# The edges between the stages of a graph network kernel: starts, gaps and the end of its four stages rearranged, and matmuls added that no one reads

## The chip, the cores and the metric

The kernel runs on one core of a Trainium2 chip. The metric is the device time of one execution in microseconds (us), as the median of three runs. The engines are TensorE (PE, with PEld for its weight loads), VectorE (DVE), ScalarE (ACT), GpSimd (POOL) and SyncE (SP). L359 stands for line 359 of the kernel before.

## The reference, cut to what matters

N is 4096 nodes, F 512 features, in H = 4 heads of D = 128. A layernorm with ReLU stands before each of two layers, and each layer's result is added to its input.

```python
# layer 0, both masks are adj
h  = relu(layernorm(x))
Xw = einsum('hnd,hde->hne', heads(h), W)
f1, f2 = Xw @ V[:, 0], Xw @ V[:, 1]
att = softmax over the neighbours of sigmoid(f1[:, :, None] + f2[:, None, :])
Xn  = batchnorm(att @ Xw)
emb = batchnorm(elu(Xn @ Wenc.T + b) + Xn)             # encoder MLP
Yc  = elu((att @ heads(emb)) @ W.T)                    # decoder attention
x   = x + batchnorm(elu(Yc @ Wdec.T + b) + Yc)         # decoder MLP
# layer 1
h = relu(layernorm(x))
feats = einsum('nf,hfo->hno', h, W1)
e_s, e_n = feats @ a_self, feats @ a_neigh
attn = softmax over the neighbours of leaky_relu(e_s[:, :, None] + e_n[:, None, :], 0.2)
x = x + relu(attn @ feats + b)
```

## The kernel before, in words

Everything but the masks (one byte) is float32 and lies transposed, features on the 128 partitions, nodes along the free axis. The stages follow one another: layernorm and projection of layer 0, encoder attention, encoder MLP, products that turn the encoder's result into values (L648), decoder attention, decoder MLP, layernorm and projection of layer 1, and the attention of layer 1 ("gat").

*Attention.* The loop at L313 runs over 8 blocks, for each head h over two halves tb of 2048 target nodes. Inside a block it runs over 32 key blocks j of 128 source nodes. For each j a weight tile `e` of 128x2048 is made from a row of scores and a mask tile and multiplied with the values of head h: four 512-column products into four banks of PSUM (L359). A product is two records in the profile, so one j is eight. The fourth bank is still being read at a block's start, so its products of j=0 and 1 are caught up at j=2 (`EVICT`, L356). In the encoder and the decoder `e` is made by ScalarE's tanh (L435) and exp (L436) and VectorE's product with the mask (L437). In the layer-1 attention it is ScalarE's Relu (L833) and one VectorE instruction (L834). The encoder writes every fifth `e` to DRAM (`KEEP`) and the decoder reads these back instead of making them (L333).

*Pools of weight tiles.* A tile `e` comes from one of two pools. Two buffers (`EP`) are in the pool `keep`, which lives from the first stage to the end of the decoder's attention. The rest are in the pool of the stage, opened when the memory of the stage before is given back: 6 in the encoder, 4 in the decoder, 7 in layer 1 (where both names stand for the stage's own pool). Which pool the next tile comes from is counted by `made`:

```python
            made += 1
            if made % (EP + ebufs) < EP:
                return keep.tile([P, TB], FP, name="e", tag="ek", bufs=EP)
            return spool.tile([P, TB], FP, name="e", bufs=ebufs)
```

*Row sums.* The softmax's denominators are sums of `e` over j. Some tiles are added by VectorE (L379, L381), some by DMAs that accumulate (L373, the tuple `moved`), and some by matmuls with ones on PE (L252, the tuple `by_ones`). At the block's end the sums of VectorE and of the DMAs go through L252 too. The decoder takes no sums; it reads the encoder's inverses back. In the last block the sums are inverted (L419, L420: `inv`, named `dsb` in the profile), spread over all partitions by PE (L425) and multiplied in. There j=31's products already come behind the sums (`early`).

*MLP.* `mlp_block` takes the products o by o and 512-column block ib by ib. The decoder's MLP also does the residual of layer 0 as its hook `between` says: L695 loads a tile `xt` of the input on SP's queue, L696 scales on ScalarE, L697 adds on VectorE, L699 and L701 sum the features up in `S`, L704 or L706 stores to the output. The decoder MLP's bias needs the sums of the weights, 32 one-column matmuls (L682), queued after the decoder attention.

*Projection of layer 1.* `w1x` holds the weights beside their products with the attention vectors (`pw`: 32 two-column records at L726, copied at L728). `centred(ib)` takes the mean with a matmul (L739), subtracts it (L745), makes ReLU and squares on ScalarE (L748, L749, L752) and adds the four squares (L753, one reduction). `deviation` (L759) follows, then eight groups of products (L776), whose values ScalarE copies with the deviation as factor (L781) and whose scores VectorE copies (L782). `store_rows` transposes the scores of one half on PE and writes them as rows to DRAM; `load_row` reads one back on all partitions. For the first half this stands at L790, behind the deviation of the block after.

*Before the layer-1 attention.* The maximum of the scores is taken over columns, transposed, taken again and spread with a ones-matmul (L796 to L805). ScalarE makes the exponentials of the columns `jcol` and then of the row in four parts (L812 to L815), and `rest_of_rows` (L817 to L827), queued at j=1, makes the rows for the other seven blocks.

*Order.* The Tile framework's scheduler sets each engine's order from the order of the program and simulated times of when operands are ready. `tc.issue_after` and the helper `pinned` fix that an instruction comes behind another in the same engine's queue; they add no wait between engines.

## Time and profile before

| | |
|---|---|
| median of 3 runs | 3273.88 us (3273.81 to 3275.61) |
| profiled execution | 3273.59 us, span of the records 3271.8 us |
| mean granted clock of TensorE in the span | 0.992 |

| stage (start to end, us from the span's start) | length | PE busy | DVE busy | ACT busy | clock |
|---|---|---|---|---|---|
| layernorm and projection, layer 0: 0 to 67.11 | 67.11 | 52.19 | 47.82 | 49.89 | |
| encoder attention: to 1053.58 | 986.47 | 951.56 | 944.35 | 960.32 | 0.99 |
| encoder MLP: to 1165.15 | 111.57 | 110.92 | 74.13 | 49.84 | |
| value products, L648: to 1194.63 | 29.48 | 29.48 | 25.13 | 4.03 | |
| decoder attention: to 2083.54 | 888.91 | 886.36 | 518.81 | 814.03 | 0.99 |
| decoder MLP: to 2193.40 | 109.86 | 109.86 | 87.42 | 66.03 | |
| norm and projection, layer 1: to 2338.64 | 145.24 | 135.01 | 82.95 | 82.29 | 0.95 |
| layer-1 attention: to 3254.12 | 915.48 | 909.87 | 886.19 | 568.00 | 0.99 |
| end: to 3271.8 | 17.68 | 10.97 | 9.13 | 5.63 | 0.93 |

The stages are cut at PE's records: a stage begins with its first matmul. The busy times are those of each engine inside the stage, and the clock is the mean that the throttle granted to PE (1.00 is full speed). The gap before a stage lies in the row of the stage before.

### The profile page before, as it was taken

How to read it: one execution, taken by the hardware profiler on the slowest of the kernel's cores; microseconds unless marked ns; L12 is line 12 of the kernel's file. 1: busy time of each engine (PE TensorE's matmuls, PEld its weight loads, DVE VectorE, ACT ScalarE, POOL GpSimd, SP SyncE). 2: the span in 40 equal slices, each digit the busy share in tenths (PEclk: the TensorE clock that was granted, in tenths of full speed). 3: DMA queues.
4: the chain of work that ended last, by engine and by line, in shares of the span. 5: the costliest groups of instructions: out<-in, count | busy, mean ns of one | idle time of the engine just before them, and what ended most of it. 6: DMA issues, size and time to landing. Idle time of an engine off the chain costs nothing.

```text
span 3271.8 us, 26021 instructions
## 1 busy us (share of the span) xinstructions
PE 3196.2 (98%) x8719; PEld 1484.0 (45%) x8719; DVE 2675.9 (82%) x1916; ACT 2600.1 (79%) x1901; POOL 465.7 (14%) x622
## 2 busy tenths in 40 slices
PE   7999999999999999999999999999999999999999
PEld 6334434444444464444444444448644444444443
DVE  6999999999999665656665665586599999999997
ACT  7999999999997449999999999565666666665663
POOL 3001211211210000000000000024312222222221
PEclk9999999999999999999999999999999999999999
DMA  9998988988986023444443444232398999889985
GB/s 208 196 195 228 268 222 225 266 222 230 271 234 157 0 68 126 151 130 136 140 151 127 132 148 133 63 132 79 84 213 214 219 228 244 214 204 236 224 217 135
DMA packets 211151, 578.48 MB, mean 177 GB/s; under 512 B 25069, under 2 KB 28173, under 8 KB 195017
## 3 DMA queue, kind: packets, MB, share of 16 engines
q0 software_dynamic: 67968, 222.51, 35.9%
q1 hardware_dynamic: 126432, 293.72, 27.1%
q10 hardware_dynamic: 16616, 60.60, 4.7%
q8 instruction: 68, 1.11, 0.1%
q14 instruction: 67, 0.54, 0.0%
HBM read 377.10 MB, written 84.29 MB: 141 GB/s over the span
## 4 chain that ended last, share of the span: by engine, by line
PE 73%; DVE 10%; ACT 7%; issue 5%; DMA 5%; POOL 0%; DVEq 0%; ACTq 0%; SPq 0%; POOLq 0%
PE ps L359 58%; PE ps L592 7%; DVE e L437 6%; ACT e L435 4%; PE ps L776 3%; DMA a<-mask 3%; ACT e L436 2%; DVE acc L381 2%; DMA acc<-e 2%; PE den L252 1%; PE ps L356 1%; PE ps L648 1%; PE ps L516 1%; DMA rinvs<-dcol 1%; PE ps L498 0%
## 5 line engine op out<-in xcount | busy, mean ns | idle before, releaser
L359 PE MATMUL ps<-e,R 128*128 128x512 f32 x6048 | 2628.8, 595 | 40.3 <-DVE e L437 32.9
L359 PEld LDWEIGHTS ps<-e,R 128*128 128x128 f32 x6048 | 1147.0, 191 | 1512.8 <-issue 1420.0
L437 DVE TENSOR_TENSOR e<-e,a 128x2048 f32<-128x2048 f32 (+1 forms) x470 | 1052.4, 2261 | 381.3 <-ACT e L436 367.1
L435 ACT ACTIVATE e<-rowb,score 128x2048 f32<-128x2048 f32 (+1 forms) x470 | 912.7, 1968 | 102.1 <-PE ps L359 58.1
L436 ACT ACTIVATE e<-e 128x2048 f32<-128x2048 f32 (+1 forms) x470 | 871.0, 1880 | 6.4
L833 ACT ACTIVATE e<-rowb,nq,jcol 128x2048 f32<-128x2048 f32 x224 | 460.8, 2089 | 269.2 <-DMA w<-e 136.6
L834 DVE SCALAR_TENSOR_TENSOR e<-e,jcol,a 128x2048 f32<-128x2048 f32 (+1 forms) x259 | 593.0, 2332 | 10.8 <-ACT e L833 10.8
L381 DVE TENSOR_TENSOR acc<-acc,e 128x2048 f32<-128x2048 f32 x130 | 297.3, 2287 | 2.1
L381 DVE TENSOR_TENSOR R<-R,e 128x2048 f32<-128x2048 f32 x121 | 278.0, 2298 | 0.0
L373 POOL DMA_DIRECT2D w<-e x178 | 150.3, 847 | 609.4 <-DMA w<-e 383.3
L592 PE MATMUL ps<-R,w 128*128 128x512 f32 x512 | 220.3, 592 | 0.6 <-DVE w L550 0.6
L373 POOL DMA_DIRECT2D acc<-e x144 | 120.4, 880 | 540.8 <-DMA acc<-e 222.9
L277 POOL DMA_DIRECT2D rb<-rinvs x60 | 34.2, 574 | 1062.5 <-DVE R L540 871.6
L592 PEld LDWEIGHTS ps<-R,w 128*128 128x128 f32 x512 | 97.2, 190 | 122.7 <-issue 117.4
L776 PE MATMUL ps<-w1x,hT 128*128 128x260 f32 x512 | 118.5, 391 | 1.8 <-ACT hT L749 1.8
L612 ACT ACTIVATE ex<-ps,bias 128x512 f32<-128x512 f32 x64 | 44.0, 687 | 95.9 <-PE ps L592 78.8
L776 PEld LDWEIGHTS ps<-w1x,hT 128*128 128x128 f32 x512 | 98.7, 194 | 21.6 <-ACT hT L749 3.4
L833 ACT ACTIVATE e<-w,nq,jcol 128x2048 f32<-128x2048 f32 (+1 forms) x35 | 65.7, 1938 | 30.8 <-DMA R<-e 30.8
L614 DVE SCALAR_TENSOR_TENSOR ex<-ex,re 128x512 f32<-128x512 f32 x64 | 45.0, 704 | 36.1 <-ACT re L613 35.9
L781 ACT ACTIVATE R<-ps,rstd 128x128 f32<-128x128 f32 x128 | 38.3, 369 | 38.1 <-PE ps L776 37.0
L787 POOL TENSOR_TENSOR vacc<-vacc,R 128x128 f32<-128x128 f32 x120 | 53.0, 468 | 57.5 <-ACT R L781 57.5
L252 PE MATMUL den<-e,ones 128*32 128x512 f32 x440 | 53.0, 598 | 0.0
(162 smaller groups left out, 1228.6 us busy)
## 6 DMA issues: line engine op xcount, KB each, us to landing
a<-mask SPq DMA_DIRECT2D x720, 256.0 KB, 4.3
w<-e POOLq DMA_DIRECT2D x178, 512.0 KB, 6.6
acc<-e POOLq DMA_DIRECT2D x144, 512.0 KB, 7.0
ekeep<-e ACTq DMA_DIRECT2D x48, 1024.0 KB, 7.4
e<-ekeep SPq DMA_DIRECT2D x48, 1024.0 KB, 4.9
mask<-in_adjT POOLq DMA_DIRECT2D x8, 2048.0 KB, 104.5
rowb<-rows SPq DMA_DIRECT2D x16, 1024.0 KB, 8.0
rb<-rinvs POOLq DMA_DIRECT2D x60, 256.0 KB, 4.5
```

What stands on the lines that cost most here:

```text
L252: last_ones = nc.tensor.matmul(den[s * 32:(s + 1) * 32, :], ones[:, 0:32], t[:, s * IB:(s + 1) * IB], start=start, stop=stop)
L359: last_main = nc.tensor.matmul(b, block(values[h], j), e[:, s * IB:(s + 1) * IB], start=(j == 0), stop=(j == NJ - 1))
L373: nc.gpsimd.dma_start(into_half, e_half, **({"accum_op": ALU.add} if j > moved[0] else {}))
L381: nc.vector.tensor_add(acc, acc, e)
L435: nc.scalar.activation(e, rowb, AF.Tanh, bias=column(score[:, 1], j, h), scale=0.5)
L436: last_act = nc.scalar.activation(e, e, AF.Exp, scale=0.5)
L437: last_dve = nc.vector.tensor_mul(e, e, a)
L592: nc.tensor.matmul(z, w[:, fb, o * P:(o + 1) * P], nodes(src[fb], ib), start=(fb == 0), stop=(fb == C - 1))
L776: nc.tensor.matmul(b[:, 0:2 * DX], hT[:, fb, c * P:(c + 1) * P], w1x[:, fb, 2 * k:2 * k + 2, :].rearrange("p h x -> p (h x)"), start=(fb = ...
L787: nc.gpsimd.tensor_add(vacc[:, h, :], vacc[:, h, :], block(v1[h], j))
L833: last_act = nc.scalar.activation(e, rowb, AF.Relu, bias=column(nq, j, h), scale=column(jcol, j, h))
L834: last_dve = nc.vector.scalar_tensor_tensor(e, e, column(jcol2, j, h), a, ALU.add, ALU.mult)
```

## The change

In the order of the program:

- *Kernel's start.* The statistics of the first 128 nodes are finished by themselves (`deviations(0, 1)`), those of the other three chunks of the first block behind the second chunk's turn.
- *Weight tiles.* With `made - 1` in place of `made`, the first two tiles of every stage come from `keep`, where before only the first did. In the first block of the decoder, j < 8, each j's weights are queued behind the exp (L436) of the j before it.
- *Decoder MLP's bias.* L682 becomes a hook of the decoder attention, queued at j=6 of its second block, and the subtraction at j=16.
- *Gap before layer 1's projection.* L726 is queued behind the MLP's last product, and a matmul of 512 columns (`stay_busy`, whose result is not read) follows each of its four groups. For block 0 the mean is taken of `S` without the last head, and a second matmul adds that head. The first two chunks' products are queued before the deviation, and `centred` of the next block comes one chunk later in block 0.
- *Rest of the projection.* L753 becomes two additions. The first half's rows are stored at chunk 2 of block 4 instead of before block 4. The residuals of head 3 are pinned behind the ReLUs of the block before.
- *Gap before the layer-1 attention.* For the last chunk the scores are copied before the values. The maximum's matmuls and the four of L821 get fillers of 256 and 512 columns behind them. One part of the row is made before the weights, the other three between the parts of the first weights, and the first three tiles are made in four parts (`in_parts0=3`).
- *End.* In the last layer-1 block j=30 and 31 are added by VectorE (L381) instead of L252, and the products of both (`late`) come behind the sums and the inverse. In the encoder's last block only j=31's products come behind the sums, as before.

The diff, with the line of the kernel before at each place and blank lines and comments left out:

```diff
@@ before 68
-GAT_LAST = (3, 5, 7, 9, 11, 13, 15, 17, 19, 21, 23), (12, 30, 31)
+GAT_LAST = (3, 5, 7, 9, 11, 13, 15, 17, 19, 21, 23), (12,)
@@ before 109
+    def stay_busy(behind, n=1, cols=IB):
+        for _ in range(n):
+            with tc.issue_after(behind.ins):
+                behind = nc.tensor.matmul(bank()[:, 0:cols], ident, w0Ts.rearrange("p h d -> p (h d)")[:, 0:cols],
+                                          start=True, stop=True)
+        return behind
@@ before 213
-                  kept=None, sums=None, sums2=None, extras={}, row0=None, masks0=()):
+                  kept=None, sums=None, sums2=None, extras={}, row0=None, masks0=(), in_parts0=1):
@@ before 242
-            if made % (EP + ebufs) < EP:
+            if (made - 1) % (EP + ebufs) < EP:
@@ before 318
-            po, ahead = [bank() for _ in range(SB - 1)], []
+            po, ahead, late = [bank() for _ in range(SB - 1)], [], []
@@ before 325
-                with pinned([a_load, *products_of] if j else []):
+                with pinned([a_load, *products_of, last_main] if j else []):
@@ before 340
-                    products_of = weights(e, rowb, a, j, h, SB if n + j == 0 else 1)
+                    with pinned(products_of[:1] if kept == "read" and n == 0 and j < 8 else []):
+                        products_of = weights(e, rowb, a, j, h, SB if NJ * n + j < in_parts0 else 1)
@@ before 364
-                early = last and j == NJ - 1 and invert is not None
-                if not early:
+                if last and invert is not None and j >= NJ - (1 if kept is not None else 2):
+                    late.append((j, e))
+                else:
@@ before 395
-                if early:
-                    products()
@@ before 409
+            for s, b in enumerate(po):
+                for k, t in late:
+                    nc.tensor.matmul(b, block(values[h], k), t[:, s * IB:(s + 1) * IB], start=(k == 0),
+                                     stop=(k == NJ - 1))
@@ before 473
+                rstd = work.tile([P, C], FP, name="rstd")
@@ before 475
-                with pinned([first_hn] if ib == 1 else []):
-                    for c in range(C):
+                def deviations(lo, hi):
+                    with pinned([first_hn] if ib == 1 or lo == 1 else []):
+                        for c in range(lo, hi):
@@ before 478
-                for c in range(C):
+                    for c in range(lo, hi):
@@ before 480
-                rstd = work.tile([P, C], FP, name="rstd")
-                last_dve = rsqrt(rstd, mv[:, :, 1], LN_EPS)
+                    return rsqrt(rstd[:, lo:hi], mv[:, lo:hi, 1], LN_EPS)
+                last_dve = deviations(0, 1 if ib == 0 else C)
@@ before 483
+                    if ib == 0 and c == 1:
+                        last_dve = deviations(1, C)
@@ before 592
-                    nc.tensor.matmul(z, w[:, fb, o * P:(o + 1) * P], nodes(src[fb], ib),
+                    last = nc.tensor.matmul(z, w[:, fb, o * P:(o + 1) * P], nodes(src[fb], ib),
@@ before 593
+                return last
@@ before 609
-                        product(z, o, ib, 0, C)
+                        last_product = product(z, o, ib, 0, C)
@@ before 622
-                last = bn_coefs(stats, gamma, beta, a_mlp, b_mlp, o, o + 1)
-            return last
+                bn_coefs(stats, gamma, beta, a_mlp, b_mlp, o, o + 1)
+            return last_product
@@ before 666
+        def sums_of_weights(load):
+            banks.append(bank1())
+            for o in range(C):
+                for fb in range(C):
+                    nc.tensor.matmul(banks[1][:, o:o + 1], w[:, fb, o * P:(o + 1) * P], ones[:, 0:1],
+                                     start=(fb == 0), stop=(fb == C - 1))
+        def bias_of_decoder(load):
+            nc.vector.tensor_sub(bias, vec_of("dec_mlp_b"), banks[1][:, 0:C])
@@ before 670
-                      kept="read")
+                      kept="read", extras={(1, 6): sums_of_weights, (1, 16): bias_of_decoder})
@@ before 679
-        pb = bank1()
-        for o in range(C):
-            for fb in range(C):
-                nc.tensor.matmul(pb[:, o:o + 1], w[:, fb, o * P:(o + 1) * P], ones[:, 0:1],
-                                 start=(fb == 0), stop=(fb == C - 1))
-        nc.vector.tensor_sub(bias, vec_of("dec_mlp_b"), pb[:, 0:C])
@@ before 697
-            nc.vector.tensor_add(d, d, xt)
+            added = nc.vector.tensor_add(d, d, xt)
@@ before 700
-            elif o > 1:
+            elif o == C - 2 or o == C - 1 and ib > 0:
@@ before 706
+            return added
@@ before 715
-        last_coefs = mlp_block(work, w, xd, x1, "dec_mlp_bn_gamma", "dec_mlp_bn_beta", None,
+        last_product = mlp_block(work, w, xd, x1, "dec_mlp_bn_gamma", "dec_mlp_bn_beta", None,
@@ before 722
+        last_pe = last_product
@@ before 723
+            with tc.issue_after(last_pe.ins):
@@ before 726
-                nc.tensor.matmul(pw[:, k:k + 2], w1Ts[:, h, fb * P:(fb + 1) * P], a1s[:, h, :], start=True, stop=True)
-        with tc.issue_after(last_coefs.ins):
-            nc.vector.tensor_copy(w1x[:, :, :, D:DX], pw[:, 0:2 * C * H].rearrange("p (c h s) -> p c h s", h=H, s=2))
+                    last_pe = nc.tensor.matmul(pw[:, k:k + 2], w1Ts[:, h, fb * P:(fb + 1) * P], a1s[:, h, :],
+                                               start=True, stop=True)
+            last_pe = stay_busy(last_pe)
@@ before 737
-            residual(C - 1, ib)
+            added = residual(C - 1, ib)
@@ before 738
+            if ib == 0:
+                with tc.issue_after(last_pe.ins):
+                    nc.tensor.matmul(pm, mean_of, S[ib], start=True, stop=False)
+                nc.tensor.matmul(pm, mean_of, nodes(x1[C - 1], ib), start=False, stop=True)
+                with tc.issue_after(added.ins):
+                    nc.vector.tensor_copy(w1x[:, :, :, D:DX],
+                                          pw[:, 0:2 * C * H].rearrange("p (c h s) -> p c h s", h=H, s=2))
+            else:
@@ before 749
-                nc.scalar.activation(hT[:, fb, :], d[:, fb, :], AF.Relu)
+                last_relu = nc.scalar.activation(hT[:, fb, :], d[:, fb, :], AF.Relu)
@@ before 753
-            nc.vector.tensor_reduce(S[ib], sq.rearrange("p c n -> p n c"), AX.X, ALU.add)
-            return hT
+            nc.vector.tensor_add(sq[:, 0:2, :], sq[:, 0:2, :], sq[:, 2:4, :])
+            nc.vector.tensor_add(S[ib], sq[:, 0, :], sq[:, 1, :])
+            return hT, last_relu
@@ before 764
-        hT = centred(0)
+        def values(hT, c):
+            banks = []
+            for k in range(2):
+                banks.append(bank())
+                for fb in range(C):
+                    m = nc.tensor.matmul(banks[k][:, 0:2 * DX], hT[:, fb, c * P:(c + 1) * P],
+                                         w1x[:, fb, 2 * k:2 * k + 2, :].rearrange("p h x -> p (h x)"),
+                                         start=(fb == 0), stop=(fb == C - 1))
+            return banks, m
+        hT, last_relu = centred(0)
+        ahead = [values(hT, c) for c in range(2)]
+        with tc.issue_after(ahead[-1][1].ins):
@@ before 769
-                if c == 1 and ib < NIB - 1:
-                    hT_next = centred(ib + 1)
+                if c == (1 if ib else 2) and ib < NIB - 1:
+                    with pinned([last_relu]):
+                        hT_next, last_relu = centred(ib + 1)
+                if (ib, c) == (SB, 2):
+                    store_rows(rows1[0], targets(0))
+                    row0 = w.rearrange("p c f -> p (c f)")
+                    load_row(row0, rows1[0], 0)
@@ before 772
+                pvs, pvs_last = ahead.pop(0) if ahead else values(hT, c)
@@ before 774
-                    b = bank()
-                    for fb in range(C):
-                        nc.tensor.matmul(b[:, 0:2 * DX], hT[:, fb, c * P:(c + 1) * P],
-                                         w1x[:, fb, 2 * k:2 * k + 2, :].rearrange("p h x -> p (h x)"),
-                                         start=(fb == 0), stop=(fb == C - 1))
-                    pv = heads_of(b)
+                    pv = heads_of(pvs[k])
+                    at_end = j == NJ - 1
+                    if at_end:
+                        nc.vector.tensor_scalar_mul(scores_of(j, k), pv[:, :, D:DX], r)
@@ before 781
+                    if not at_end:
@@ before 790
-            if ib == SB - 1:
-                store_rows(rows1[0], targets(0))
-                row0 = w.rearrange("p c f -> p (c f)")
-                load_row(row0, rows1[0], 0)
+        last_pe = stay_busy(pvs_last, cols=IB // 2)
@@ before 798
-        nc.tensor.transpose(pt[0:H, 0:P], mloc, ident)
+        with tc.issue_after(last_pe.ins):
+            last_pe = stay_busy(nc.tensor.transpose(pt[0:H, 0:P], mloc, ident), cols=IB // 2)
@@ before 804
-        nc.tensor.matmul(pm[:, 0:H], ones[0:H, :], mdiag, start=True, stop=True)
+        with tc.issue_after(last_pe.ins):
+            last_pe = nc.tensor.matmul(pm[:, 0:H], ones[0:H, :], mdiag, start=True, stop=True)
@@ before 809
-        last_act = nc.scalar.activation(jcol, jcol, AF.Exp)
-        nc.vector.tensor_scalar_mul(nq, jcol2, -1.0)
+        last_exp = nc.scalar.activation(jcol, jcol, AF.Exp)
@@ before 812
-        for row, in in_parts(SB, row0):
-            last_dve = nc.vector.tensor_scalar(row, row, mbc[:, 0:1], G_MAX, ALU.add, ALU.min)
-            with tc.issue_after(last_act.ins):
-                last_act = nc.scalar.activation(row, row, AF.Exp, scale=0.8)
+        row_parts = [row for row, in in_parts(SB, row0)]
+        def held(row):
+            nc.vector.tensor_scalar(row, row, mbc[:, 0:1], G_MAX, ALU.add, ALU.min)
+        held(row_parts[0])
+        last_scalars = nc.vector.tensor_scalar_mul(nq, jcol2, -1.0)
@@ before 817
-    def rest_of_rows(load):
@@ before 819
+    with tc.issue_after(last_pe.ins):
@@ before 821
-            nc.tensor.matmul(pss[:, h:h + 1], vacc[:, h, :], ones[:, 0:1], start=True, stop=True)
+            last_pe = nc.tensor.matmul(pss[:, h:h + 1], vacc[:, h, :], ones[:, 0:1], start=True, stop=True)
+    last_pe = stay_busy(last_pe, 3)
+    def rest_of_rows(load):
@@ before 831
+        last_act = last_exp
@@ before 832
+            if row_parts:
+                row = row_parts.pop(0)
+                with tc.issue_after(last_act.ins), tc.issue_after(last_scalars.ins):
+                    if len(row_parts) < SB - 1:
+                        held(row)
+                    nc.scalar.activation(row, row, AF.Exp, scale=0.8)
@@ before 860
+        with tc.issue_after(last_pe.ins):
@@ before 863
-                  (N * TINY, ALU.add), sums=R[2][:, 0:TB], sums2=(row0, R[2][:, TB:N]), row0=row0,
+                      (N * TINY, ALU.add), sums=R[2][:, 0:TB], sums2=(row0, R[2][:, TB:N]), row0=row0, in_parts0=3,
```

## The prediction

> **What bounds the kernel now.** I read the page's first part, then TensorE's (PE's) timeline, the granted clock in short stretches, then VectorE's (DVE's) timeline.
>
> ```profile
> PE 3196.2 (98%) x8719; PEld 1484.0 (45%) x8719; DVE 2675.9 (82%) x1916; ACT 2600.1 (79%) x1901; POOL 465.7 (14%) x622
> ```
>
> PE is busy 98% of the span, so only its 75.6 us of idle time, its stretches at half clock and work taken off it can move the end. The timeline of PE says where these lie (start, length, instruction, count, idle time before it):
>
> ```profile
> 1194.63 2.74 PE L359 MATMUL ps<-e,R 128*128 128x512 f32 x6
> 1197.20 1.02 PE L356 MATMUL ps<-e,R 128*128 128x512 f32 x2
> 1198.06 4.39 PE L682 MATMUL den<-ones,w 128*128 128x1 f32 x32
> 1205.01 5.46 PE L359 MATMUL ps<-e,R 128*128 128x512 f32 x6 [2.55 <-DVE e L437]
> 1210.26 1.37 PE L356 MATMUL ps<-e,R 128*128 128x512 f32 x2
> 1211.47 108.31 PE L359 MATMUL ps<-e,R 128*128 128x512 f32 x252
> ...
> 2193.40 3.63 PE L726 MATMUL den<-a1s,hT 128*128 128x2 f32 x32
> 2201.17 2.04 PE L739 MATMUL ps<-S,mean_of 128*128 128x512 f32 x2 [4.14 <-DVE S L701]
> 2205.02 6.75 PE L776 MATMUL ps<-w1x,hT 128*128 128x260 f32 x16 [1.80 <-ACT hT L749]
> ...
> 2242.65 1.05 PE L759 MATMUL den<-mean_of,S 128*128 128x1 f32 x8 [2.23 <-DVE S L753]
> ...
> 3257.70 3.70 PE L359 MATMUL ps<-e,R 128*128 128x512 f32 x8
> 3261.97 3.70 PE L425 MATMUL ps<-dsb,ident 128*128 128x512 f32 x8 [0.57 <-DVE dsb L420]
> ```
>
> A 512-column matmul is two records of 0.429 us at full clock (252 in 108.2) and twice that at half clock. One key block j of an attention stage is 8 records, 3.43 us. The stretches by window give the clock (second last columns: PEclk, DMA share):
>
> ```profile
> 309.84:313.25 3.41, 1.51 (x4) 0.49 (x3) 3.41 (x4) 3.41 (x3) 0.00 (x0) 1.00 0.00 1
> 794.54:797.95 3.41, 1.61 (x5) 0.68 (x4) 3.41 (x2) 3.41 (x3) 0.00 (x0) 1.00 0.77 317
> 1197.31:1200.72 3.41, 3.41 (x28) 2.93 (x26) 0.00 (x0) 3.41 (x3) 0.00 (x0) 1.00 0.93 332
> 1204.14:1207.55 3.41, 2.54 (x3) 1.17 (x4) 2.92 (x2) 3.41 (x3) 0.00 (x0) 0.50 0.25 79
> ```
>
> The clock falls at 74.3, 313.3, 965.2, 1200.7, 2197.4 and 2340.8 us and rises at 81.2, 316.7, 968.6, 1211.0, 2211.1 and 2351.0. All differences are multiples of 3.413 us (2340.8-1200.7 is 334 of them), so it is decided in windows of that length. PE counted as fully busy in the third window and lost the clock: 2.6 us of it were one-column matmuls. With 1.61 us of 512-column work (the window at 794.54) it held; with 1.51 it fell. A cold window with 2.54 us did not raise it. So only columns streamed count, about 1.5 of 3.41 us hold the clock, and nearly a full window restores it.
>
> Last, VectorE's supply in the layer-1 attention:
>
> ```profile
> 2452.76 11.41 DVE L834 SCALAR_TENSOR_TENSOR e<-e,jcol,a 128x2048 f32<-128x2048 f32 x5
> 2458.91 1.92 PE L252 MATMUL den<-e,ones 128*32 128x512 f32 x16
> ```
>
> The first of these five is block 0's last weight tile, j=31, ready at 2455.1. PE starts on it at 2458.91-3.43, about 2455.4. VectorE is busy for all 103 us from 2356 to 2459. Its lead, some 4 to 5 us at j=20, is down to 0.3 us: PE cannot end this block earlier than VectorE lets it.
>
> **The change part by part**, on the profiled execution's own time, 3273.59 us (span 3271.8); the median is 0.29 above it.
>
> *Decoder attention's start, +4.8.* Two tiles instead of one now come first from the pool that outlives the encoder stage. In the changed program's order ScalarE makes j=1, not j=5, right after the encoder attention (where 1049.5 to 1053.4 held j=5). So both j=0 and j=1 wait ready at 1194.63. ScalarE then makes j=2 from 1194.8: tanh 1.94, exp 1.9, VectorE's mask product 2.3, ready 1201.0; PE wants it at 1194.63+16x0.429=1201.5. j=3 is ready at 1204.9 and wanted at 1204.9; from j=5 on there are 3 us to spare. The order pinned over j<8 keeps ScalarE from pairing tanhs there. Gain: 1211.47-1201.5=9.97. But L682 hid in this gap, and is now queued on PE behind block 1's j=5, in a stage that PE bounds without a gap. Its price by L726, 32 such records in 3.4: 3.45 us. Then the clock: L555's 24 small records (3.04 us from 962.7) lost it for one window, so I add half of 3.41, 1.7. 9.97-3.45-1.7=4.8. Bounds: no clock lost 6.5; two windows and a late j=3, 2.5.
>
> The Trainium skill, "TensorE: Matmul & The Clock Gate", Part 1, says that the clock follows how busy PE has been in free-running windows of some 3.4 us, and advises that no idle gap exceed about 3 us. The grid agrees, at 3.413. By PE's busy row, L682 would keep the clock and the part be worth 6.5; by the window at 1197.31 small matmuls are as good as idle. I follow the trace.
>
> *Gap before layer 1's projection, +3.1.* L726 is cut into four groups of 8 records (0.86 each) with a 512-column filler (0.86) after each: PE runs to 2193.4+6.9=2200.3. All four lie in the wait of 4.14, and half of the stretch streams, 1.6 to 1.7 us per window, barely above the 1.5 that fell. The mean (L739) now takes S without head 3 and then x1[3] itself, dropping VectorE's L701 (0.69) from the chain: one more matmul, both at full clock, done 2202.0. VectorE subtracts from 2202.15 (was 2203.26). ScalarE has one residual (L696) ahead of the first ReLU, not eight, so L776 starts near 2203.6. Sixteen L776 matmuls (0.44 each) follow before the deviation; the squares are added in 1.2+0.7 (between the 0.69 and 2.29 of 512 and 2048 columns). I place block 1's first L776 at 2221.7, against 2225.28: 3.6. In the wait from 2202 to 2206 only three 0.44 us matmuls stream; a window lying there (one phase in three) loses the clock, 0.5 on average. Bounds 1.5 and 4: if the fillers fail to hold the clock they cost nothing, lying in the wait.
>
> *Rest of layer 1's projection, +2.6.* L753's reduction (3.75 us, which PE waited for at 2242.65, 2.23) becomes two adds of 1.9. The transpose of the first half's scores waits no more (0.39 at 2275.6). PE's own period is 15.78 us a block; ScalarE has 11.3, VectorE 8.6 in it. The residuals of blocks 4 to 7 move inside their blocks; on SP the row load now stands between the loads of xt, with a full block of slack. Bounds 0 and 3.
>
> *Gap before layer 1's attention, +1.15.* The last score goes ahead of ScalarE's copies (mloc 0.66 earlier), one row part is finished before the first weights, and the first three key blocks are split in four. First product: 2342.5 against 2344.90. But ScalarE now runs 4 row exps at 0.52, 12 parts at 0.71 and g: from 2340.4 to 2351.2 instead of 2341.0 to 2350.2, so j=3 leaves VectorE 0.9 earlier only (start 2353.3 against 2354.19), because VectorE no longer waits for L821 and the transpose after it (1.16 before 2351.56). From there its queue is full to j=31. PE gains 0.9 and the lead of 0.26. By the skill's rule the gap must not cool PE: 6.1 us at half clock, another 3.05, and the total would be 17.5. By the lead these are handed back as waits for e before j=31; I take 1.15. Bounds 0 and 4.5. Fillers here lie in a wait of 4.99.
>
> *End, +2.6.* The row sums of j=30 and 31 go from L252 (16 records, 1.74) to two more VectorE adds (2x2.23); VectorE ended its last tile at 3241.9, so they are done by 3246.4, five us before the sums. Two products, 6.87 us, now follow the sums, over the inverse's 0.69+3.35: the 0.57 wait and 0.26 of slack go. 1.74+0.83=2.57. Bounds 2 and 2.8.
>
> *Kernel's start, 0.* The first chunk's statistics are finished alone, so its transposes start near 6.4 instead of 9.5; chunks 1 to 3 then follow the second, separate chain, at 9.75, as before. Bounds -1.7 (the clock rises a window later) and +0.5. The encoder attention is unchanged: ScalarE is 99.9% busy there.
>
> Sum 14.3: 3273.88-14.3=3259.6.
>
> **The rivals.** *The fillers decide the second gap* (chance 0.12): PE keeps its 4.5 us. For it: PE was cold for 6 us. Against: the lead. 3256.
> *New waits eat most* (0.10): j=3 late, the clock lost twice, the fillers too sparse. For it: margins of 0.1 us. About 3267.
> *Slower* (0.03): SP's queue holds the residual loads of each block behind stores and the row load, and with two xt tiles the mean waits in every block of the projection. It decides above (11.7+6.5)/7=2.6 us a block; one wait for xt of 2.50 is in the trace (VectorE, 2231.7), hidden there. At 3.5 a block it is 24.5-11.7: 3287. Against: a block of slack.
> *The change does not do what it says*: cold PE in both gaps despite the fillers leaves 12 or 13 of the 14.3; it stays in the main case (0.75), 3255 to 3265.
>
> **How the numbers follow.** 0.2% is 6.5 us, about what can be told from no change. Faster: 0.75+0.12+half of the 0.10, 0.92 with rounding; same 0.05; slower 0.03. The range, 3254.5 to 3265.0, is the main case with most of the first rival.
>
> **What would show it.** Right: L359 unbroken from 1194.6; L682 inside block 1 with the clock falling once after it; L753 gone and no wait at its place; waits for VectorE's e before the end of the first layer-1 block. Wrong: that block without a wait and over 3 us shorter, waits for xt, or a gap at j=3 of the decoder.

## The result, and the profile after

| | before | after |
|---|---|---|
| median | 3275.74 us, 13 runs (3272.27 to 3279.27) | 3265.74 us, 13 runs (3260.23 to 3269.86) |
| ratio | | 0.9968, 95% interval 0.9961 to 0.9975 |
| profiled execution, span | 3273.59, 3271.8 | 3260.23, 3258.4 |

The change saves 10.0 us between the medians; the ratio gives 10.5, with an interval of 8.2 to 12.8. The prediction was 14.3 us and 3259.6, with a range to 3265.0. The direction was right, the size too large, and the time came out 0.7 us above the range. The profiled execution of after is the shortest of its 13, so the 13.4 us between the two profiles flatter the change; a second profile of each follows below.

The page of after, first part:

```profile
PE 3197.5 (98%) x8723; PEld 1484.0 (46%) x8723; DVE 2665.4 (82%) x1933; ACT 2601.8 (80%) x1908; POOL 477.6 (15%) x622
```

PE's busy time has grown by 1.3 us, its idle time has fallen from 75.6 to 60.9 us, and the span has shrunk by 13.4. (A record at half clock counts twice as long in the busy time, so the added fillers and the cold windows that went, windows of 3.413 us at half clock, nearly cancel in it.) PE's timeline in after, at the decoder attention's start and at the moved sums (L371 is the product, L368 the catch-up, L694 the sums):

```profile
1196.54 5.32 PE L371 MATMUL ps<-e,R 128*128 128x512 f32 x12
1201.69 1.88 PE L368 MATMUL ps<-e,R 128*128 128x512 f32 x4
1203.40 17.49 PE L371 MATMUL ps<-e,R 128*128 128x512 f32 x40
1222.21 18.29 PE L371 MATMUL ps<-e,R 128*128 128x512 f32 x42 [1.32 <-DVE e L452]
...
1328.75 3.63 PE L694 MATMUL den<-ones,w 128*128 128x1 f32 x32
1332.24 13.12 PE L371 MATMUL ps<-e,R 128*128 128x512 f32 x30
```

The gap of 2.55 us after j=0 and the sums in it are gone, but a wait of 1.32 us stands five tiles later, before j=7. The gap before layer 1's projection, the gap before its attention, and the end:

```profile
2196.72 1.11 PE L115 MATMUL ps<-w0Ts,ident 128*128 128x512 f32 x2
2197.66 1.02 PE L771 MATMUL ps<-S,mean_of 128*128 128x512 f32 x2
2198.52 1.02 PE L772 MATMUL ps<-x,mean_of 128*128 128x512 f32 x2
2200.98 7.31 PE L809 MATMUL ps<-w1x,hT 128*128 128x260 f32 x32 [1.44 <-ACT hT L787]
...
2330.14 4.52 PE L115 MATMUL ps<-w0Ts,ident 128*128 128x512 f32 x6
2334.49 5.31 PE L371 MATMUL ps<-e,R 128*128 128x512 f32 x12
...
2439.97 3.70 PE L371 MATMUL ps<-e,R 128*128 128x512 f32 x8 [0.76 <-DVE e L904]
2444.44 3.70 PE L371 MATMUL ps<-e,R 128*128 128x512 f32 x8 [0.77 <-DVE e L904]
...
3241.70 7.13 PE L423 MATMUL ps<-e,R 128*128 128x512 f32 x16
3248.68 3.60 PE L440 MATMUL ps<-dsb,ident 128*128 128x512 f32 x8
```

The wait of 4.14 us for the mean is gone and the clock stays up through the fillers (L115), as the same profile's windows from the MLP's last product on show (1.00, third column from the end):

```profile
2190.65:2197.66 7.01, 7.01 (x41) 5.09 (x40) 5.37 (x13) 3.57 (x5) 0.00 (x0) 1.00 0.00 0
2197.66:2208.00 10.34, 8.90 (x37) 6.54 (x36) 5.51 (x8) 5.08 (x9) 0.00 (x0) 1.00 0.20 71
```

In the layer-1 attention PE starts earlier (7.3 us behind the projection's end instead of 7.6, and 5.6 in the second profile, which lost no window there) and then waits twice for VectorE's last tiles of the block, as the prediction said. At the end the two late products run into the spreading without a wait.

The lengths of the stages, from PE's records of all profiles taken (the encoder attention ends with its last product, the two decoder blocks with the third block's catch-up, and the last stretch with the span). "Before" means every profile whose code in that stage is that of the kernel before, "after" likewise; the number of profiles is in brackets.

| stretch | before, mean (range) | after, mean (range) | gain | predicted |
|---|---|---|---|---|
| start, to the encoder's first product | 69.8 (67.1 to 74.7) [6] | 69.3 (68.2 to 71.6) [11] | none clear | 0 |
| encoder attention | 983.6 (982.4 to 985.9) [4] | 984.7 (982.0 to 987.2) [9] | -1.1 | 0 |
| decoder attention, first two blocks | 233.9 (233.3 to 234.9) [3] | 231.9 (230.2 to 233.6) [9] | 2.0 | 4.8 |
| MLP's end to the projection's end | 144.1 (142.6 to 145.2) [5] | 136.4 (136.35 to 136.5) [10] | 7.8 | 5.7 |
| projection's end to the second layer-1 block's catch-up | 129.5 (128.9 to 130.4) [5] | 129.74 (129.73 to 129.75) [7] | -0.2 | 1.15 |
| last layer-1 block's catch-up to the end | 120.25 [5] | 117.7 [12] | 2.55 | 2.57 |

All other stretches agree to 0.01 us from kernel to kernel (the six layer-1 blocks between take 683.82 us in each). The gains sum to 11.0 us, which lies within the interval of the ratio. The ranges of the encoder attention overlap, so its -1.1 is not clear by itself.

### The profile page after: what moved, and what is told of

Same layout as the page of the kernel before. It is cut to its first block, busy times and chain, and to the rows that moved or that the text cites. A ratio compares the mean times of both kernels' runs of the same rounds, so it can differ in the third digit from the quotient of the medians.

```text
span 3258.4 us, 26085 instructions
## 1 busy us (share of the span) xinstructions
PE 3197.5 (98%) x8723; PEld 1484.0 (46%) x8723; DVE 2665.4 (82%) x1933; ACT 2601.8 (80%) x1908; POOL 477.6 (15%) x622
## 4 chain that ended last, share of the span: by engine, by line
PE 68%; ACT 12%; DVE 9%; issue 7%; DMA 3%; POOL 0%; ACTq 0%; DVEq 0%; POOLq 0%
PE ps L371 52%; ACT e L450 7%; PE ps L613 7%; DVE e L452 5%; ACT e L451 4%; PE ps L809 3%; DMA a<-mask 2%; DVE acc L394 2%; PE den L262 1%; DVE e L904 1%; DVE R L394 1%; PE ps L670 1%; DMA acc<-e 1%; PE ps L368 1%; PE ps L537 1%
## 5 line engine op out<-in xcount | busy, mean ns | idle before, releaser
L371 PE MATMUL ps<-e,R 128*128 128x512 f32 x6024 | 2614.1, 594 | 37.5 <-DVE e L452 35.2
L371 PEld LDWEIGHTS ps<-e,R 128*128 128x128 f32 x6024 | 1140.1, 190 | 1504.8 <-issue 1396.6
L613 PEld LDWEIGHTS ps<-R,w 128*128 128x128 f32 x512 | 97.2, 190 | 122.7 <-issue 117.7
L846 POOL TENSOR_TENSOR vacc<-vacc,R 128x128 f32<-128x128 f32 x120 | 65.8, 576 | 45.3 <-ACT R L839 45.0
```

What stands on the lines that cost most here:

```text
L371: last_main = nc.tensor.matmul(b, block(values[h], j), e[:, s * IB:(s + 1) * IB], start=(j == 0), stop=(j == NJ - 1))
L613: last = nc.tensor.matmul(z, w[:, fb, o * P:(o + 1) * P], nodes(src[fb], ib), start=(fb == 0), stop=(fb == C - 1))
L846: nc.gpsimd.tensor_add(vacc[:, h, :], vacc[:, h, :], block(v1[h], j))
```

## The experiments

"Before" runs on the same chip beside every group, and its median differs from chip to chip, so kernels of one group are compared with each other or by their ratio to before.

**The changed kernel again, and the kernel before again.** No edit.

> The changed kernel as it is. Its profile of 3260.23 us is the lowest of its 13 times (median 3265.74), so the 13.4 us between the two profiles are more than the 10.0 between the medians. Theory A (phase): the clock's 3.413 us windows lie differently in each execution; this trace then shows other half-clock windows, mostly at the kernel's start, near 962, after L694 and in the two gaps, each worth up to 1.7 us, and they make up the difference to the first profile; everywhere else the stages agree within 0.3 us. Theory B (supply): the difference lies in the encoder attention, whose blocks 0 to 3 already differ by -1.1 to +0.4 us between the two profiles; then the clock's windows explain under 1 us of it and the blocks before 580 us explain the rest. Expected time 3263 to 3268 us under both.

> The kernel before as it is, for a second profile of it. Theory A (phase): start, gaps and the small-matmul places carry other half-clock windows than the first profile, the encoder's blocks agree within 0.3 us. Theory B (supply): the encoder's first blocks differ by about 1 us each, the stages from 1170 us on agree within 0.3 us apart from single windows of 1.7. Expected 3273 to 3278 us.

Measured: after 3266.01 us (6 runs, 3263.85 to 3266.71; before 3275.1), its profiled execution 3266.62. The 6.4 us between the two profiles of after lie in three places: the encoder attention took 986.4 instead of 982.0, the second decoder block 115.14 instead of 113.44 (one cold window), the rest at the start. So both theories hold a part, and supply holds the larger one. Before's second profile (3273.2) has 983.1 us in the encoder, and 1.6 us less in the decoder's start and 1.4 less before the layer-1 attention than its first: two cold windows in each where the first had three. The prediction had measured its gains against a profile with these extra windows.

**The old start.** `deviations(0, C)` for every block, so that all four statistics come together.

> The changed kernel with only the kernel's start as before (all four statistics of the first block together). In the first profile of the changed kernel the clock rose at 20.2 us instead of 12.9 and the encoder attention began at 69.38 instead of 67.11. Theory A: the split start does this, since its first transposes leave a wait of 2.06 us on PE and no window is full; then this kernel begins the encoder attention near 67.1 and is 1.9 to 2.3 us faster than the changed kernel. Theory B: the window's phase does it; then the begin lies anywhere between 66.5 and 69.5 in both, and the times differ by under 1 us.

Measured: 3266.31 us (6 runs) beside 3266.01 of after on the same chip; its encoder begins at 69.17 us, after's at 69.66. That is theory B, the phase; the old start reaches from 67.1 to 74.7 us in six profiles and the new one from 68.2 to 71.6 in eleven, so the split start shows neither gain nor loss. The 2.3 us that the first profile of after seemed to lose here were one execution's.

**One VectorE addition less in the first layer-1 block.**

```diff
-GAT_FIRST = (0, 2, 4, 6, 8, 10, 12, 14, 16, 18, 20, 22, 24), (30, 31)
+GAT_FIRST = (0, 2, 4, 6, 8, 10, 12, 14, 16, 18, 20, 22, 24, 26), (30, 31)
```

> The changed kernel with j=26 of the first layer-1 block summed by the DMA instead of VectorE (one 2.28 us add less there). Theory A (VectorE's lead bounds this block): the three waits of PE for e (1.8 us together, two of them near j=27 to 31) go, the stretch from the first product to the second block's catch-up (122.40 us in the changed kernel's profile) shrinks by 1.3 to 1.8 us to about 120.8, and the whole by the same. Theory B (the waits come from single tiles' latency or from the DMA sums): the stretch stays within 0.4 us, or grows because the block's sums wait for a later accumulation.

Measured: 3263.16 us (5 runs) beside 3266.01, which so few runs do not tell from chance (the means differ by 1.8); the stage's length does. PE's waits in the block, after (second profile) first and then this kernel (line, what it waited for, us in total, times, longest):

```profile
PE ps L371 <- DVE e L904: 1.8, 3, 0.8
PE ps L193 <- ACT g L890: 1.1, 1, 1.1
...
```

```profile
PE ps L193 <- ACT g L890: 1.1, 1, 1.1
...
PE ps L371 <- DVE e L904: 0.3, 1, 0.3
```

Three waits for `e` become one of 0.3, and the stretch from the projection's end falls from 129.74 to 127.54 us, 2.2 less, about the price of the 2.28 us addition and more than the 1.3 to 1.8 expected. VectorE's lead bounds this block: with the addition its queue is full from the fourth tile to the last, and PE ends when VectorE does.

**No fillers in the first gap; no fillers in the second.** `stay_busy` left out behind L755's groups, and in the other kernel all five fillers before the layer-1 attention: behind the last products, behind the maximum's transpose and behind the sums (L881).

> The changed kernel without the four fillers before layer 1's projection; nothing else differs on PE. Theory A (the fillers hold the clock there): PE's clock falls near the end of the decoder MLP's last products and comes back only about 10 us into the projection; from the MLP's end to the projection's end takes 139 to 142 us instead of 136.4. Theory B (the clock is held anyway or the stretch waits for VectorE and ScalarE): the stretch stays within 0.5 us of 136.4.

> The changed kernel without the five fillers before the layer-1 attention. Theory A (VectorE's lead decides): the clock falls for one to three windows and the first product is later or slower, but from the projection's end to the second block's catch-up still takes 129.7 to 130.2 us (129.7 and 129.8 in two profiles, of which one lost the clock there and one did not); time unchanged. Theory B (the fillers decide this gap): 1.7 to 5 us more in that stretch and in the time.

Measured: without the first, the stretch from the MLP's end to the projection's end is 138.42 us instead of 136.36, so these four fillers are worth 2.06 us by this one profile; ten profiles with them lie between 136.35 and 136.51. The medians are 3266.99 (8 runs) and, without the second, 3265.06 (4 runs); against before (ratios 0.9970 and 0.9964) neither can be told from after's 0.9968. Without the first the clock was lost for three windows (busy time by engine; the third column from the end is PE's clock):

```profile
2201.46:2204.87 3.41, 1.30 (x2) 0.50 (x2) 1.43 (x6) 1.00 (x2) 0.00 (x0) 0.50 0.00 0
2204.87:2208.28 3.41, 1.97 (x4) 0.62 (x3) 2.11 (x4) 1.36 (x3) 0.00 (x0) 0.50 0.45 154
2208.28:2211.70 3.42, 3.42 (x10) 2.65 (x9) 0.74 (x2) 3.42 (x7) 0.00 (x0) 0.50 0.00 0
```

PE was busy in 6.69 of these 10.2 us, so half clock cost 3.3 at most (an estimate, half of 6.69); the rest of them are PE's waits. Why 2.06 of the 3.3 remain was not followed. In the second gap the clock was lost as well, PE's first products ran at half speed, and nothing was lost in time:

```profile
2334.35 8.22 PE L371 MATMUL ps<-e,R 128*128 128x512 f32 x12 [2.53 <-issue]
2342.41 0.27 PE L193 MATMUL ps<-ident,g 128*128 128x128 f32 x1
2342.52 1.88 PE L368 MATMUL ps<-e,R 128*128 128x512 f32 x4
```

The same twelve records took 5.31 us in the first profile of after. Still the stretch to the second block's catch-up is 129.74 us here, and 129.73 and 129.74 in after's two profiles, of which one lost a window and one did not. The fillers of the second gap are worth nothing: what PE loses there it would otherwise wait for later.

**The old reduction.** `tensor_reduce` over the four squares in place of two additions, one run.

> The changed kernel with the squares of layer 1's norm added by the one reduction (3.75 us) instead of two additions (1.23+0.69). From the MLP's end to the projection's end 136.36 us in the changed kernel. Theory A (PE waited for this reduction): once per early block a wait of 1 to 2 us before the deviation comes back, 138.5 to 142 us. Theory B (the new place of the next block's norm and the pinned residuals already give it a block of slack): within 0.5 us of 136.4, except for block 0.

Measured: 138.42 us for the same stretch, so the two additions are worth 2.06 us. Only the first two blocks lose, with waits of 0.37 and 0.28 at block 0 and 1.19 at block 1; from block 2 on there is slack. So neither theory holds whole: the loss is near what A asked for at least, 138.5, but stands in two blocks only.

**The turn alone.** In the kernel before, `made - 1` in place of `made`, and nothing else.

> The kernel before with one edit: made - 1 in place of made, so that two tiles of every stage come from the pool that lives on. On PE only the 16 sums of the decoder's weights (L682) stand behind j=1's products now instead of j=0's. Theory A (the turn alone fills the decoder's start; the moved sums were not needed): the two first decoder blocks, from the first product to the third block's catch-up, take 2x109.87+5.15+3.45 = 228.3 us plus 1.7 per window at half clock, 228 to 232, against 234.9 and 233.3 in two profiles of before and 230.2 to 233.6 with the whole change. Theory B (without the pinned order and the moved sums a later tile is late): 232 or more. For the encoder: theory C (the turn makes its row sums' DMAs late in block 2): the whole encoder attention 982 or 986.5, with a wait of ScalarE near 317 or 340 us after its start and none near 311; theory D (execution alone): a wait near 311 again, 982.4 to 983.1. Time: A and D about 3270, A and C up to 3274.

Measured: PE's timeline at the decoder's start:

```profile
1205.96 5.32 PE L359 MATMUL ps<-e,R 128*128 128x512 f32 x12
1211.11 1.88 PE L356 MATMUL ps<-e,R 128*128 128x512 f32 x4
1212.83 3.63 PE L682 MATMUL den<-ones,w 128*128 128x1 f32 x32
1216.32 34.15 PE L359 MATMUL ps<-e,R 128*128 128x512 f32 x79
```

The two blocks take 228.46 us, 5.4 less than before and 3.4 less than the whole change has on the mean. The sums at their old place fill the time until j=2 is ready, and no window was lost behind them, here or in the other kernel with this code. So the moved sums and the pinned order do not help; they take back a good part of what the turn gives. But the median of this kernel is 3274.65 (13 runs), 1.0 below before (ratio 0.9997, 0.9989 to 1.0006). What became of the other four us was open after it. Its encoder took 986.1.

**The encoder in the old turn.** `made - (kept != "write")`: old turn in the encoder attention, new one elsewhere.

> The changed kernel, but in the encoder attention the weight tiles come from the two pools in the old turn (made instead of made - 1); the order on every engine stays. In three of four profiles with the new turn the encoder attention from its first product to its last took 986.0 to 987.2 us (the first one 982.0), in two of before 982.4 and 983.1; the difference lies in the third block (124.6 to 124.7 against 121.7 and 122.3). Theory A (the turn decides which buffers the row sums' DMAs read and hold): the encoder attention goes back to about 983, its third block to 122, and the whole to about 3262.5. Theory B (supply varies from execution to execution): 986 again as often as not, the time stays at 3265 to 3266.

Measured: 983.02 us in the encoder, a wait of ScalarE at 311 us; 3264.47 us (5 runs), in the same group as the two without fillers (3266.99 and 3265.06). By itself this does not settle it, since profiles with the new turn reach 982 too.

**A better kernel, and the same with the old encoder turn.** On top of after: j=26 by DMA, `j < 10` in place of `j < 8` for the pinned tiles, and the sums folded:

```diff
+            ws = spool.tile([P, IB], FP, name="exd", bufs=2)
+            nc.vector.tensor_add(ws, w[:, 0, :], w[:, 1, :])
+            for fb in range(2, C):
+                nc.vector.tensor_add(ws, ws, w[:, fb, :])
             for o in range(C):
-                for fb in range(C):
-                    nc.tensor.matmul(banks[1][:, o:o + 1], w[:, fb, o * P:(o + 1) * P], ones[:, 0:1],
-                                     start=(fb == 0), stop=(fb == C - 1))
+                nc.tensor.matmul(banks[1][:, o:o + 1], ws[:, o * P:(o + 1) * P], ones[:, 0:1], start=True, stop=True)
```

> The changed kernel with three edits: j=26 of the first layer-1 block summed by the DMA (as before: -2.2); the decoder's first eight tiles pinned up to j < 10, so that j=8's tanh no longer passes j=7's (PE waited 1.32 us there); and the decoder bias's weight sums folded over the four row blocks by three VectorE adds of 0.69, which lie in VectorE's slack, so that 8 one-column records are left of 32 (3.45 to 0.86 us) and the clock is not lost after them (1.7 to 3.4 in three of four profiles). Theory A: 2.2+1.3+2.6+1.7, 7.8 us less than the changed kernel, about 3258.2. Theory B: the adds delay the mask products of block 1 or another tile is late at the decoder's start; then only the 2.2 and part of the rest, about 3262.

> The three edits of the better kernel (3257.88) and, in the encoder attention alone, the old turn of the weight tiles. Theory A (the new turn costs the encoder up to 4 us in more than half of the executions): its attention takes 982.4 to 983.2 us, with a wait of ScalarE near 311 us, and the median is 1.5 to 2.5 us lower, about 3256. Theory B (execution alone): the median stays within 1 us of 3257.9, and the encoder may take 986 here too.

Measured: 3257.88 us (5 runs, ratio 0.9940, 0.9927 to 0.9952) and, with the old turn, 3257.29 (5 runs; before 3275.63). The first forecast held to 0.3 us, in part by luck, since it was set from another group's median: by the stages this kernel is 8.2 us shorter than after (5.95 in the decoder's first two blocks, 2.2 in the layer-1 block), where 7.8 were expected. PE's timeline of the better kernel:

```profile
1203.40 36.80 PE L371 MATMUL ps<-e,R 128*128 128x512 f32 x85
...
1327.16 0.95 PE L697 MATMUL den<-ones,exd 128*128 128x1 f32 x8
1327.97 7.54 PE L371 MATMUL ps<-e,R 128*128 128x512 f32 x17
```

With j=8 held back, PE runs on at j=7 without a wait: 115.18 us for the stretch that took 116.76. So the 1.32 us of after were j=8's tanh ahead of j=7's in ScalarE's queue. The folded sums take 0.8 us and lose no window: 110.76 us for the second block against 113.44 to 116.82. With the old turn the encoder took 985.9 in its profile, so it too has long executions, and the medians agree within 1 us: theory B, as far as five runs each tell.

**A lighter third encoder block.** On top of the better kernel; then the same edit in before, in the turn alone and in after.

```diff
+ENC_THIRD = (0, 2, 10, 12, 15, 17, 20, 22, 25), (5, 7, 8, 9, 30, 31)
 ENC = (0, 2, 5, 7, 10, 12, 15, 17, 20, 22, 25), (8, 9, 30, 31)
...
-lambda n: (ENC_FIRST, ENC_SECOND, ENC)[min(n, 2)]
+lambda n: (ENC_FIRST, ENC_SECOND, ENC_THIRD, ENC)[min(n, 3)]
```

> The better kernel (3257.88; its encoder turn is the new one) with a lighter third encoder block: j=5 and j=7 are summed by ones-matmuls on PE instead of the DMA (11 tiles by DMA become 9; 1.74 us more PE work in a block that ScalarE bounds). In eleven profiles so far the third block took 120.7 to 125.0 us, with either turn, and what ScalarE waits for there is the DMA of a row sum (acc<-e), 1.8 to 7.0 us in all; POOL's queue sends these one behind the other and stands 12.1 us behind the small transfer of the denominators and 7.4 to 8.4 behind that of the inverses. Theory A (these sums are late, by how long a transfer takes in that execution): the third block takes 119 to 121 us, ScalarE's waits near 311 to 341 us after the encoder's start are gone or under 1 us, and the median falls by about 2, to 3256. Theory B (the supply of masks, or ScalarE itself, sets the block): 121 to 125 us still, the median within 1 us of 3257.9.

Measured: 3251.57 us (5 runs, 3249.34 to 3252.18; before 3276.69; ratio 0.9922, 0.9908 to 0.9935), the fastest of all. By the ratios it is some 6 us below the better kernel, where about 2 were expected; with five runs of each on different chips the size is rough. What ScalarE waited for in the third encoder block, in the first and in the second profile of after:

```profile
ACT e L450 <- DMA acc<-e: 1.8, 2, 1.1
```

```profile
ACT e L450 <- DMA acc<-e: 5.7, 3, 2.8
```

With the lighter block no such wait is left, and the block takes 119.64 us (120.7 to 125.0 in thirteen profiles without the edit). POOL's queue shows where the two executions of after part, at the same pair of accumulations; the first profile, then the second:

```profile
371.06 1.84 POOL L386 DMA_DIRECT2D acc<-e  x2
378.22 0.85 POOL L386 DMA_DIRECT2D acc<-e  x1 [5.33 <-DMA acc<-e]
```

```profile
372.58 1.84 POOL L386 DMA_DIRECT2D acc<-e  x2
381.62 0.85 POOL L386 DMA_DIRECT2D acc<-e  x1 [7.19 <-DMA acc<-e]
```

The next accumulation goes only when the last has landed. Here it waits 1.9 us longer; the row sums behind it hold their weight tiles as much longer, and ScalarE, which bounds the encoder, waits for a tile.

> The kernel before with the lighter third encoder block (j=5 and 7 summed by PE instead of the DMA), as the base for two others. Both accounts: third block 119 to 121 us; time 3270 to 3273 with less spread than before's 3272 to 3282.

> The kernel before with made - 1 and the lighter third encoder block. Account 2 (the turn's cost lies in the encoder's third block): its median is 4.8 to 6.4 us, what the decoder's start gives, below that of the kernel before with the lighter third block. If the turn costs elsewhere, or the decoder's gain is not steady: 0 to 3 us below.

> The changed kernel with the lighter third encoder block. Account 1 (the sum was too large; stages outside the encoder give 11.2 on the mean of the profiles: decoder's start 1.9, gap and projection of layer 1 6.8, gap before its attention -0.1, end 2.6): its median is 10 to 12 us below that of the kernel before with the lighter third block. Account 2 (the encoder took back 3 to 4 us of 14): 13 to 15 below.

| third block light in | median | third block | whole encoder attention |
|---|---|---|---|
| before | 3270.45 (21 runs, 3267.50 to 3275.24) | 119.06 | 978.87 |
| the turn alone | 3267.61 (9 runs, 3264.51 to 3273.18) | 119.66 | 980.17 |
| after | 3260.66 (5 runs, 3257.68 to 3263.22) | 119.65 | 981.23 |

The whole change is worth 9.8 us on this base (10.4 by the means, give or take 2.6): close to the 10 to 12 of account 1, while the 13 to 15 of account 2 begin at the edge of the error. The turn is worth 2.8 by the medians (2.9 by the means, give or take 2.2), and the 4.8 that account 2 asked for at least lies just inside that error. The runs alone thus favour account 1 without closing the question. The traces show the part that goes missing. With the old turn the second encoder block took 123.87 to 124.01 us in five profiles, with the new one 124.12 to 125.64 in twelve; with the light third block that block takes 0.6 us more too. In the second block ScalarE's longest wait, some 210 us after the encoder's first product and in fifteen of the seventeen profiles for a row sum's DMA, takes 1.2 to 2.6 us in the five and 3.0 to 4.3 in the twelve. So 1.3 to 2.4 us of the encoder are the turn's own price (978.87 in one profile against 980.17 to 981.23 in two), and the 5.4 us of the decoder less this are 3.0 to 4.1, which the 2.8 measured meets within its error. One expectation failed: the lighter block did not narrow the spread of the kernel before (7.7 us in 21 runs, 7.8 in 29 of before itself on that chip).

## Why the prediction was wrong in size

- **Decoder's start: 4.8 predicted, 2.0 measured**, below the part's own lower bound of 2.5. This is the step that failed. The fill of the gap was right in kind, and so was the clock, lost for one window on the mean of nine profiles (none in two, one in five, two in two). Two terms were wrong. The gain of 9.97 rested on "The order pinned over j<8 keeps ScalarE from pairing tanhs there" and "from j=5 on there are 3 us to spare". But j=8 is not pinned, and ScalarE made its tanh right behind that of j=6 and ahead of j=7's (first profile of after; j=4 is read back):

```profile
1208.26 3.88 ACT L450 ACTIVATE e<-rowb,score 128x2048 f32<-128x2048 f32 x2
1212.05 1.89 ACT L451 ACTIVATE e<-e 128x2048 f32<-128x2048 f32 x1
1217.66 4.49 DVE L452 TENSOR_TENSOR e<-e,a 128x2048 f32<-128x2048 f32 x2 [1.40 <-ACT e L451]
```

So j=7 came last of the two products in the third line, ready at 1222.15, and PE went on at 1222.21. It cost 1.6 us, as the better kernel shows. And the baseline 1211.47 belonged to an execution with three cold windows, where the other two profiles of before have two (1 us on the mean). The price of the moved sums, 3.45, was nearly right (113.44-109.87=3.57); that they had to be paid was the change's, not the prediction's, doing. These terms make the sum: 9.97-1.6-0.9-3.57-1.7 is 2.2, against 2.0.
- **Encoder attention: 0 predicted, -1.1 measured** (-1.3 to -2.4 with the third block light). "ScalarE is 99.9% busy there" held for the stretch from 400 to 710 us, and was taken for the whole. In the kernel before, ScalarE was busy 77.34 and 77.03 of 80 us in the two stretches ahead of it (fourth of the engines):

```profile
240.00:320.00 80.00, 77.13 (x187) 33.02 (x186) 79.83 (x45) 77.34 (x43) 13.04 (x18) 0.98 0.83 237
320.00:400.00 80.00, 80.00 (x223) 33.99 (x222) 73.23 (x43) 77.03 (x42) 17.19 (x23) 1.00 0.91 253
400.00:710.00 310.00, 299.94 (x786) 127.05 (x785) 300.73 (x166) 309.71 (x168) 56.40 (x73) 1.00 0.87 234
```

ScalarE's idle time in those two, 5.6 us, was nearly all waits for row sums, and the turn of the buffers changed which tile it waits for. Why the new turn waits longer was not tried.
- **Gap before the layer-1 attention: 1.15 predicted, -0.2 measured.** The mechanism was right, with its waits at the block's end where they were foretold. Against the profile that the sum was made on, 0.65 us came (130.39 to 129.74); but that one had three cold windows here, the other four with the old code two (128.9 to 129.5 us), and against these nothing is gained. The rival that let the fillers decide is refuted by the kernel without them. The Trainium skill's advice against long gaps ("TensorE: Matmul & The Clock Gate", Part 1, which puts the limit at some 3.4 us) would have made the total 17.5 by the prediction (14.3 and 3.05 are 17.35). On the clock it points the right way, since the clock did fall without fillers, though no idle gap there was longer than 2.53 us; heeding it bought no time here.
- **Gap and projection of layer 1: 5.7 predicted, 7.8 measured**, above the two upper bounds of 4 and 3 together. The first product of block 1, in before and in the first profile of after:

```profile
2225.28 3.75 PE L776 MATMUL ps<-w1x,hT 128*128 128x260 f32 x16
2218.11 3.75 PE L809 MATMUL ps<-w1x,hT 128*128 128x260 f32 x16
```

From L726's first record (2193.40, in after 2190.65) that is 31.88 and 27.46 us, so the gap gave 4.4 for 3.1; from there to the projection's end the gain is 3.0 for 2.6, and 0.3 is the mean of five profiles against the one. Of the excess in the gap 0.5 is the clock, which the fillers held; the other 0.8 was not followed. By the kernels without them the fillers give 2.06 and the two additions 2.06; what is left, 3.6, falls to the mean without head 3, the earlier products and the moved residuals, which were not run by themselves.
- **End: 2.57 predicted, 2.55 measured. Start: 0 and none clear.**
- **The rivals.** "New waits eat most", at about 3267, came nearest to the 3265.74 measured, though its late tile was j=3 and the late one was j=7, and the fillers were not too sparse. The loads of `xt` of the rival "slower" did not come late: VectorE waited 0.5 us for one of 32 in the first profile of after.

The terms together are off by 3.3 us. The time itself is off by 6.1: 1.9 of this is the base (the median of before was 3273.88 in three runs and 3275.74 in thirteen), 3.3 the terms, and 1.0 what the medians show less than the mean lengths of the stages. That the terms are not further off is luck: the other parts fell short by 5.3, and the projection's excess of 2.1 made part of it good. The range of 10.5 us held the sizes of the steps but not the spread of this kernel, 9.6 us in thirteen runs of one program. Two sources of that spread are seen in the profiles: windows of the clock (1.7 us each), and the encoder's third block (120.7 to 125.0). They are not all of it, since with that block light the kernel before spreads over 7.7 us still.

## What to carry to other kernels

Take a second profile of the kernel before, if there is one, before subtracting microseconds: a grid of clock windows that starts at another place in each execution, and transfers that land early or late, make single traces differ by as much as a change of this size. Before crediting a filled gap, ask which other engine's queue is full from there on: fillers before the projection paid where PE hardly waits behind them, and those before the layer-1 attention paid nothing where VectorE is the bound. And in this kernel, work that fits into a gap was better left in it (5.4 us instead of 2.0), while small matmuls that had to move were better made fewer than hidden (110.76 us for the block instead of 113.44 to 116.82).

## What the runs showed of the hardware

Whether a burst of one-column matmuls costs the clock goes with the phase of the 3.413 us windows: in nine profiles with the same code there, the same 32 records (3.45 us) stood in a stage without other idle time and lost no window in two, one in five and two in two. In the first profile of after the burst began 1.26 us into a window, so that 2.15 us of it lay in that window and 1.26 us of wide products were left there; the next window kept the clock (1.00, third column from the end):

```profile
1327.49:1330.90 3.41, 3.41 (x25) 2.69 (x23) 1.87 (x2) 3.38 (x3) 0.00 (x0) 1.00 0.29 83
1330.90:1334.31 3.41, 3.41 (x19) 2.37 (x19) 1.87 (x2) 2.42 (x2) 0.00 (x0) 1.00 0.29 77
```

In the second profile it began 2.09 us into one, so that 2.17 us lay in the window after it and 1.24 us of wide products were left there; the next one is cold, with PE fully busy in both:

```profile
1334.74:1338.15 3.41, 3.41 (x24) 2.82 (x24) 1.87 (x2) 3.25 (x2) 0.00 (x0) 1.00 0.15 36
1338.15:1341.57 3.42, 3.42 (x5) 1.35 (x4) 2.20 (x1) 0.00 (x0) 0.00 (x0) 0.50 0.17 55
```

The other profiles fit: 1.14 us of wide products or less lost the next window, 1.56 kept it. So the border lies near 1.25 us of 3.41 here, where the prediction had put it at 1.5 from two windows in the encoder (1.51 lost, 1.61 held); why the two places differ is open. Two windows were lost where the burst began 0.26 and 0.40 us into one (the old start and the encoder in the old turn): its last 0.64 and 0.91 us then lay in the first cold window, and a second followed.
